# Attention and routed experts in one kernel: unordered stores, moved sums, and a new filling of the steps

## The chip, the cores and the metric

The kernel runs on one core of one Trainium2 chip. The metric is the device time of one execution in microseconds (us). Five engines run their own queues in order: TensorE (PE, with its weight loads as PEld), VectorE (DVE), ScalarE (ACT), GpSimd (POOL) and SyncE (SP, which here only issues DMAs). They wait for each other through semaphores.

## The reference

x has the shape (4, 1024, 512); there are 16 heads of 32, and 8 experts of rank 64. All is float32. B, the experts' second matrix, has the shape (8, 512, 64), A (8, 64, 512).

```python
q, k, v = x @ wq.T, x @ wk.T, x @ wv.T          # in 16 heads, no scaling of the scores
a = softmax(q @ k^T) @ v                        # over 1024 keys, each batch and head
x = layernorm(x + a @ wo.T)
logits = x @ Wr.T + br                          # 8 experts
e, w = argmax(softmax(logits)), max(softmax(logits))
y = (x @ A[e].T) @ B[e].T / 64                  # the chosen expert alone
x = layernorm(x + y * w)
```

## The kernel before

**Steps.** A unit is one batch and one group of four heads, 16 units. The kernel is a written list of 272 steps (and a rest that runs after them). In step i, `scores(i)` takes four matmuls of 128 queries by 512 keys, one head each, for a unit that is 16 steps (`NS`) ahead of the one weighed; DVE takes the maximum of each (L321), and for half of the rows, in the odd steps, ACT also sums the exponentials (L324, one pass over 512 columns for each head). `weigh(i - 16)` computes transposed scores for two blocks of 128 keys and 256 queries: first the row maximum (and, where the sum is known, its logarithm's counterpart for the division) is put into the banks by matmuls of three bf16 parts (L370), then the scores are added (L379), then ACT writes the exponentials, `probs` (L389). Four such steps (`KP`) cover the 1024 keys of 256 queries; in the last of them, a "busy" step (i % 4 == 3), `combine` multiplies with v (L431).

**Two ways to the sum.** Of each eight steps (`TS`), the first four (i % 8 < 4) have no sums from `scores`: GpSimd adds up `probs` into `dens` (L394, L397, eight parts, 2.36 us each), and four steps after the product `settle` sums over the partitions with a matmul by ones (L405), divides (L406) and multiplies (L408). The other four steps (`summed_early`) take the sums of the exponentials that ACT made during `scores`: `pick` matmuls spread the inverse (L417), it is copied to `inv` (L425), and the product is multiplied with it (L440). Both fall in steps 7 mod 8, `settle` first. At the end of the eight `scores` steps the maxima are gathered (L335 to L337: a reduction, a subtraction and an exponential of 16 columns), in the next step `invert` makes the inverse (L343 to L345) and GpSimd splits it into three bf16 parts; two steps later `turn_m` transposes it (L352).

**Banks.** All PE results go through eight PSUM banks in a ring (`bank()`): a step takes four for `weigh`, four for `scores`, one for each piece. A matmul waits until the last reader of its bank is done.

**Pieces.** Projections (q, k, v: L283, L293, L302; output: L503), expert steps and the dense feed-forward of the last batch are pieces with a cost, a first and a last step. A planner walks through the steps and takes pieces, those that are due first, until the step's length passes a level; the level was 1500 above the mean in i % 4 == 1 and 750 below it elsewhere. Work that follows a piece is put into later steps with `later` (small work, after `scores` and `combine`, ahead of the pieces). After the list is made, `keep_order` fixes each engine's order as written.

**After attention.** For batches 0 to 2 (`After`), the normed rows are sorted by expert: `choose` and `gate` find the expert, `count` (L556 to L600) each row's place, `scatter` (GpSimd, indirect DMA, L604, eight for each batch) writes the rows to `sorted` in DRAM. Ten expert steps follow, each with up to three parts of different pairs of tiles: `turn_tokens` (L649), `up` (L656), `down` (L665). SP loads tokens and the expert's matrices (`load_tokens` L620, `load_up` L634, `load_down` L639). Then `weigh_y` takes statistics, GpSimd norms (`apply`, L468), and `store` writes the rows to their places in `out` by an indirect DMA from GpSimd (L683, 48 in all). The framework orders two DMAs that write the same DRAM tensor, so each store waits for the one before it. The last batch (`Last`, L739 to L781, four groups of 256 rows) computes all experts densely with a mask, and SP stores it (L791).

Short names below: steps have the matmuls T1 (L370), T (L379), S (L319), AV (L431), set (L405); o is a piece of the output projection; tt, eu, ed are the three parts of an expert step; lt, l1, lu, lm, ld are the last batch's transposes, mask transposes, up, mask and down.

Of the kernel before, what the change touches and what calls it, by code (L numbers as in the profile page):

```python
# [41 lines left out]
def attention_then_experts(  # L42
# [263 lines left out]
    def scores(s):  # L306
# [24 lines left out]
        if here == TS - 1:  # L331

            m = spread_from[i % 2]
            less = work.tile([P, TQ, GH, 2], F32, tag="less", name="less")
            dve.tensor_reduce(m[:, :, :, 0], top[i], axis=AX.X, op=ALU.min)  # L335
            dve.tensor_sub(less, m[:, TQ:, :, 0:1].to_broadcast((P, TQ, GH, 2)), top[i][:, TQ:])
            act.activation(less, less, AF.Exp)  # L337
            room[i] = m, less
# [23 lines left out]
    def weigh(s):  # L362
# [27 lines left out]
        if not summed_early(s):  # L390
            now = [pr[:, k].rearrange("p j q -> p (j q)") for k in range(2)]
            if kp == 0:
                dens[u, c] = work.tile([P, GH * QC], F32, tag="dens", name="dens", bufs=1)
                pool.tensor_add(dens[u, c], now[0], now[1])  # L394
            else:
                for w in now:
                    pool.tensor_add(dens[u, c], dens[u, c], w)  # L397

    def settle(s):
# [4 lines left out]
        for j in range(GH):  # L404
            pe.matmul(ps[j * HD : (j + 1) * HD, :], ones, dens[u, c][:, ts(j, QC)], start=True, stop=True)  # L405
# [4 lines left out]
    def combine(s):  # L410
# [3 lines left out]
        if summed_early(s):  # L414
# [10 lines left out]
            dve.tensor_copy(inv, ps)  # L425
# [73 lines left out]
    def add_projection(b, n, i, half, h, raw):  # L499
# [6 lines left out]
        if half:  # L506
            dve.tensor_add(raw[:, i], ps[:, H2:], vS[b, 1][:, n * TQ + i, H2:])

    class After:
# [107 lines left out]
        def load_tokens(self, k):  # L617
            for i in range(2):
# [61 lines left out]
        def store(self, k):  # L680
            for i in range(2):
                t = self.x[k, i]
                pool.indirect_dma_start(  # L683
# [6 lines left out]
                )  # L690
# [12 lines left out]
    class Last:  # L703
# [26 lines left out]
        def norm(self):  # L730
            for i in range(TQ):
                apply(self.h[i], self.rs, i, pool if self.n < NQ - 1 else act)
# [55 lines left out]
        def finish(self):  # L788
            self.norm()
            for i in range(TQ):  # L790
                sync.dma_start(out[B - 1, ts(TQ * self.n + i, P), :], self.h[i])  # L791
# [6 lines left out]
    SHORTEST = 8800  # L798
    pieces, loads = [], {}
# [21 lines left out]

    def start_of(u):
        return NS * (u + 1)

    for i in range(len(weights)):
# [3 lines left out]
        if kp == KP - 1:  # L829
            base[i + NS] += COST_AV + (QC + 4 * QC if summed_early(i) else 0)  # L830
# [5 lines left out]
    for i in range(len(weights) // TS):  # L836
        later(TS * i + TS, 0, invert, i, where=ahead)
        later(TS * i + TS + 2, 512, turn_m, i)
# [38 lines left out]
    for b, r in enumerate(rest):  # L877
# [7 lines left out]
        for t in range(NT):  # L885
            n, i = divmod(t, TQ)
            for half in range(2):
                then = []
                if i == TQ - 1 and half == 1:
                    then = [(1, 0, r.norm, n), (3, 0, r.choose, n), (4, 0, r.gate, n)]  # L890
                    if n == NQ - 1:
                        then += [(4, 600, r.count)]
                        then += [(5 + k // 4, 0, r.scatter, k) for k in range(NT)]
# [9 lines left out]
        for k in range(NT + 2):  # L903
# [3 lines left out]
                end + 12 + 3 * k,  # L907
                end + (20 + 4 * k if b < B - 2 else 19 + 3 * k),
                after=[(p, 3 if k else 9)],
# [13 lines left out]
    for n in range(NQ):  # L923
        a = start_of(LAST) + NS * n + NS - 1
        p, ups, downs = None, [], []
        for i in range(TQ):
            for half in range(2):
                then = []
                if i == TQ - 1 and half == 1:
                    gap = 1  # L930
                    then = [(gap, 0, on_last(n, "norm")), (gap + 1, 2200, on_last(n, "turn"))]
                    then += [(gap + 1, 0, on_last(n, "choose")), (gap + 2, 0, on_last(n, "weigh"))]
                    then += [(gap + 2, 300, on_last(n, "turn_one"))]
# [9 lines left out]
        for k in range(C):  # L943
            ups.append(Piece(on_last(n, "up", k), HALF, a + 4, a + 12, after=[(p, gap + 2)]))
        q = Piece(on_last(n, "mask"), 1024, a + 6, a + 14, after=[(p, gap + 3)] + [(o, 1) for o in ups])
# [10 lines left out]
    for i in range(len(base)):  # L956
# [23 lines left out]

        level += 1500 if i % KP == 1 else -750
        length = base[i]
        while True:
# [8 lines left out]
            for gap, cost, f, *args in p.then:  # L992
                later(i + abs(gap), cost, f, *args, where=ahead if gap < 0 else small)
# [16 lines left out]
    for r in rest:  # L1010
        for k in range(NT):
            early[r.steps[k].step - 2].append(lambda r=r, k=k: r.load_tokens(k))
# [26 lines left out]
    for i in range(len(base)):  # L1039
# [8 lines left out]
        if i in busy:  # L1048
            if summed_early(i - NS):
# [45 lines left out]
```

## Time and profile before

| | |
|---|---|
| median of 3 runs | 1541.05 us (1538.18 to 1541.54) |
| profiled execution | 1541.39 us; its span 1539.4 us, mean granted clock 0.989 |
| PE busy | 1493.6 us (97%) |
| DVE, ACT, POOL busy | 1008.9, 946.4, 772.3 us |
| largest groups on DVE, ACT, POOL | L321 maxima 636.1; L389 exponentials 529.2, L324 347.8; L397 additions 452.8 |
| HBM | 92.34 MB read, 33.63 MB written, 82 GB/s over the span |

A profile's instruction row reads: start, busy time, engine, line, operation, what it writes <- what it reads, partitions x elements, count; in brackets the engine's idle time ahead of it and what ended that. A PE matmul of float32 stands as two records. In the waits view a row names who waited for whom: total us, times, longest. Idle time on an engine that nobody waits for costs nothing.

### The profile page before, as it was taken

To read this page: it belongs to the slowest core of one execution; us is meant where nothing else is said; L and a number is where in the kernel's file an instruction comes from. 1 tells how busy PE (TensorE), PEld (TensorE's weight loads), DVE (VectorE), ACT (ScalarE), POOL (GpSimd) and SP (SyncE) were. 2 spreads that over 40 slices of the span, in tenths; PEclk is the share of its full clock that TensorE was granted. 3 is DMA by queue.
4 is the path that set the end of the run, shared out by engine and by line. 5 is a ranking of instruction groups with operands and counts; after the bars stand their busy time and mean duration, and the time that the engine had idled before them with its cause. 6 is when DMAs were issued, how large, how long until landed. Compare 5 with 4: busy or idle time off the path is not lost.

```text
span 1539.4 us, 37695 instructions
## 1 busy us (share of the span) xinstructions
PE 1493.6 (97%) x14899; PEld 972.3 (63%) x14899; DVE 1008.9 (66%) x2117; ACT 946.4 (61%) x2267; POOL 772.3 (50%) x809
## 2 busy tenths in 40 slices
PE   8999999999999999999999999999999999989997
PEld 6676666666665656666666666666666666656665
DVE  3766666666776667677777657777776667776523
ACT  1346677767665676766665676766565577666651
POOL 2013444444556345666644546665555645477651
PEclk9999999999999999999999999999999999999999
DMA  6422121223001513422111513342500231231000
GB/s 233 138 94 72 56 84 43 70 94 114 2 1 49 173 47 114 133 81 98 29 56 37 177 57 90 108 148 64 165 15 28 93 102 36 75 108 34 20 11 28
DMA packets 93056, 122.12 MB, mean 79 GB/s; under 512 B 7607, under 2 KB 68039, under 8 KB 92880
## 3 DMA queue, kind: packets, MB, share of 16 engines
q1 hardware_dynamic: 84672, 103.93, 21.3%
q0 software_dynamic: 6096, 13.69, 2.4%
q8 instruction: 117, 1.92, 0.5%
q10 hardware_dynamic: 2112, 2.10, 0.4%
q14 instruction: 59, 0.48, 0.1%
HBM read 92.34 MB, written 33.63 MB: 82 GB/s over the span
## 4 chain that ended last, share of the span: by engine, by line
PE 85%; ACT 5%; issue 4%; DVE 2%; POOL 2%; DMA 1%; SPq 0%; ACTq 0%; POOLq 0%; DVEq 0%
PE bank L431 15%; PE bank L319 14%; PE bank L379 14%; PE bank L283 8%; PE bank L302 8%; PE bank L293 8%; PE bank L503 6%; PE bank L370 5%; ACT probs L389 4%; PE bank L762 2%; PE bank L777 1%; ACT junk L324 1%; PE bank L665 1%; PE bank L656 1%; POOL dens L397 1%
## 5 line engine op out<-in xcount | busy, mean ns | idle before, releaser
L321 DVE TENSOR_REDUCE top<-bank 128x1 f32<-128x512 f32 x1024 | 636.1, 683 | 318.3 <-PE bank L319 303.4
L389 ACT ACTIVATE probs<-bank 128x512 f32<-128x512 f32 x1024 | 529.2, 605 | 414.0 <-PE bank L379 405.9
L397 POOL TENSOR_TENSOR dens<-dens,probs 128x1024 f32<-128x1024 f32 x192 | 452.8, 2358 | 86.0 <-ACT probs L389 77.1
L324 ACT ACTIVATE junk<-bank,top 128x512 bf16<-128x512 f32 x512 | 347.8, 717 | 76.1 <-DVE top L321 75.9
L319 PE MATMUL bank<-k,q 32*128 32x512 f32 x2048 | 316.2, 600 | 2.5 <-DVE whose_i L600 1.2
L379 PE MATMUL bank<-q,k 32*128 32x256 f32 x4096 | 274.4, 378 | 1.1 <-issue 1.1
L431 PE MATMUL bank<-probs,v 128*32 128x256 f32 x4096 | 237.9, 384 | 4.7 <-ACT probs L389 3.9
L211 POOL CAST sm<-sf 128x32 bf16<-128x32 f32 x32 | 8.2, 256 | 423.5 <-DVE sf L345 404.0
L379 PEld LDWEIGHTS bank<-q,k 32*128 32x128 f32 x4096 | 204.8, 186 | 22.8 <-issue 7.5
L431 PEld LDWEIGHTS bank<-probs,v 128*32 128x32 f32 x4096 | 128.3, 111 | 114.3 <-ACT probs L389 32.3
L319 PEld LDWEIGHTS bank<-k,q 32*128 32x128 f32 x2048 | 129.3, 186 | 37.2 <-DVE aT L440 6.9
L283 PE MATMUL bank<-xT,wq 128*128 128x256 f32 x512 | 130.8, 402 | 10.4 <-DMA xT<-in_xt 7.6
L283 PEld LDWEIGHTS bank<-xT,wq 128*128 128x128 f32 x512 | 96.5, 197 | 53.3 <-ACT probs L389 23.7
L293 PE MATMUL bank<-xT,wk 128*128 128x256 f32 x512 | 125.2, 389 | 0.3 <-ACT probs L389 0.3
L503 PE MATMUL bank<-wo,aT 128*128 128x264 f32 (+1 forms) x512 | 122.7, 390 | 2.4 <-ACT probs L389 2.4
L302 PE MATMUL bank<-wv,xT 128*128 128x256 f32 (+1 forms) x512 | 124.4, 391 | 0.0
L370 PE MATMUL bank<-mT,ones_b 3*128 3x512 bf16 x1024 | 115.7, 386 | 6.1 <-ACT junk L324 5.0
L324 ACT ACTIVATION_READ_ACCUMULATOR junk<-bank,top 128x1 f32 x512 | 121.5, 237 | 0.0
L302 PEld LDWEIGHTS bank<-wv,xT 128*128 128x128 f32 x512 | 93.8, 190 | 38.4 <-ACT probs L389 22.1
L293 PEld LDWEIGHTS bank<-xT,wk 128*128 128x128 f32 x512 | 95.2, 191 | 35.9 <-ACT probs L389 22.4
L503 PEld LDWEIGHTS bank<-wo,aT 128*128 128x128 f32 x512 | 94.2, 190 | 37.0 <-ACT probs L389 22.9
L370 PEld LDWEIGHTS <-ones_b 3*128 3x128 bf16 x1024 | 28.6, 91 | 97.8 <-issue 97.2
(137 smaller groups left out, 1142.9 us busy)
## 6 DMA issues: line engine op xcount, KB each, us to landing
xT<-in_xt SPq DMA_DIRECT2D x98, 512.0 KB, 4.0
sorted<-nothing SPq DMA_DIRECT2D x12, 1028.0 KB, 6.6
x<-sorted SPq DMA_DIRECT2D x48, 257.0 KB, 2.8
h<-in_x SPq DMA_DIRECT2D x32, 256.0 KB, 7.4
wa<-in_wa SPq DMA_DIRECT2D x48, 128.0 KB, 2.1
wb<-in_wb SPq DMA_DIRECT2D x48, 128.0 KB, 3.7
out<-h SPq DMA_DIRECT2D x8, 256.0 KB, 3.6
wv<-in_wv ACTq DMA_DIRECT2D x2, 512.0 KB
```

The costliest lines, as they stand in the source:

```text
L283: pe.matmul(ps, wq_sb[:, c, ts(units[u][1], P)], x.x[:, c, :], start=(c == 0), stop=(c == C - 1))
L293: pe.matmul(ps, wk_sb[:, c, ts(units[u][1], P)], x.x[:, c, :], start=(c == 0), stop=(c == C - 1))
L302: pe.matmul(ps, x.x[:, c, ts(t, P)], wv_sb[:, c, columns(h)], start=(c == 0), stop=(c == C - 1))
L319: pe.matmul(ps, q[r, ts(t % TQ, P)], kT[u][r, ts(n, 512)], start=True, stop=True)
L321: dve.tensor_reduce(top[i][:, at, j, n : n + 1], ps, axis=AX.X, op=ALU.max, negate=True)
L324: act.activation(junk[:, j % 2, :], ps, AF.Exp, bias=top[i][:, at, j, n : n + 1], accum_out=sums[i][:, at - TQ, j, n : n + 1],)
L370: pe.matmul(ps.rearrange("p (k q) -> p k q", q=QC), ones_b[r, :], m[r, :].unsqueeze(1).to_broadcast((NP, 2, QC)), start=True, stop=False,)
L379: pe.matmul(ps[:, ts(k, QC)], kT[u][r, ts(2 * kp + k, P)], qT[u, c][r, :], start=False, stop=(k == 1),)
L389: act.activation(pr[:, :, j, :], ps.rearrange("p (k q) -> p k q", q=QC), AF.Exp)
L397: pool.tensor_add(dens[u, c], dens[u, c], w)
L431: pe.matmul(ps[j * HD : (j + 1) * HD, :], v[:, k, col : col + HD], probs[u, c, k // 2][:, k % 2, j, :], start=(k == 0), stop=(k == NK - 1),)
L503: pe.matmul(ps, aT[b, c, n][:, ts(i, P)], wo_sb[:, c, columns(half)], start=(c == 0), stop=(c == C - 1))
```

## The change

- `store` and `finish` declare that no store to `out` depends on another one.
- The gathering of the maxima and sums becomes `gather`, put into the step's small work: behind `settle` and `combine` on every engine's queue.
- `inv` is copied by ACT instead of DVE.
- The scatters are put two to a step, into steps in which GpSimd adds nothing.
- In the last 256 queries of the last batch, GpSimd adds six of the eight parts; `settle` takes the other two by matmuls of its own (12 instead of 4) and runs one step after the product.
- The planner's level is a fixed 10900 in steps 1 mod 4 (room for two pieces) and the mean elsewhere.
- Expert steps start 5 steps later (ends and gaps change too), their tokens are loaded one step ahead instead of two; in the last batch the transposes come 2 or 3 steps after the projection instead of 2, and the norms of its third group go from GpSimd to ACT.

```diff
-        if here == TS - 1:
-
-            m = spread_from[i % 2]
-            less = work.tile([P, TQ, GH, 2], F32, tag="less", name="less")
-            dve.tensor_reduce(m[:, :, :, 0], top[i], axis=AX.X, op=ALU.min)
-            dve.tensor_sub(less, m[:, TQ:, :, 0:1].to_broadcast((P, TQ, GH, 2)), top[i][:, TQ:])
-            act.activation(less, less, AF.Exp)
-            room[i] = m, less
+    def gather(i):
+
+        m = spread_from[i % 2]
...
+        room[i] = m, less
...
-                for w in now:
+                for w in now[: added(u, c) - 2 * kp]:
                     pool.tensor_add(dens[u, c], dens[u, c], w)
+
+    def added(u, c):
+
+        return NK if u < LAST or c < NQ - 1 else NK - 2
...
-        for j in range(GH):
-            pe.matmul(ps[j * HD : (j + 1) * HD, :], ones, dens[u, c][:, ts(j, QC)], start=True, stop=True)
+        others = range(added(u, c), NK)
+        tiles = [probs[u, c, k // 2][:, k % 2] for k in others]
+        tiles.append(dens[u, c].rearrange("p (j q) -> p j q", q=QC))
+        for w in tiles:
+            for j in range(GH):
+                pe.matmul(
+                    ps[j * HD : (j + 1) * HD, :], ones, w[:, j, :], start=(w is tiles[0]), stop=(w is tiles[-1])
+                )
...
-            dve.tensor_copy(inv, ps)
+            act.copy(inv, ps)
...
+    stores = []
+
+    def stored(i):
+
+        for other in stores:
+            tc.declare_no_dep(i, other, reason="other rows")
+        stores.append(i)
...
-                pool.indirect_dma_start(
+                i = pool.indirect_dma_start(
                     out=out_rows,
...
-                )
+                ).ins
+                stored(i)
...
-                apply(self.h[i], self.rs, i, pool if self.n < NQ - 1 else act)
+                apply(self.h[i], self.rs, i, pool if self.n < 2 else act)
...
-                sync.dma_start(out[B - 1, ts(TQ * self.n + i, P), :], self.h[i])
+                stored(sync.dma_start(out[B - 1, ts(TQ * self.n + i, P), :], self.h[i]).ins)
...
+    HEAVY = 10900
...
+    def quiet(i, k):
+
+        for j in range(i, i + 4 * NS):
+            k -= summed_early(j)
+            if k < 0:
+                return j
...
-            base[i + NS] += COST_AV + (QC + 4 * QC if summed_early(i) else 0)
+            base[i + NS] += COST_AV
+            if summed_early(i):
+                base[i + NS] += QC
+            elif added(u, c) == NK:
+                settled_later.add(i + NS)
+                base[i + NS + KP] += 4 * QC
+            else:
+                later(i + NS + 1, 3 * 4 * QC, settle, i)
...
+        later(TS * i + TS - 1, 0, gather, i)
...
-                        then += [(5 + k // 4, 0, r.scatter, k) for k in range(NT)]
+                        then += [(lambda i, k=k: quiet(i + 5, k // 2), 0, r.scatter, k) for k in range(NT)]
...
-                end + 12 + 3 * k,
-                end + (20 + 4 * k if b < B - 2 else 19 + 3 * k),
-                after=[(p, 3 if k else 9)],
+                end + 17 + 3 * k,
+                end + (25 if b < B - 2 else 21) + 4 * k,
+                after=[(p, 3)] if k else [],
...
-                    gap = 1
-                    then = [(gap, 0, on_last(n, "norm")), (gap + 1, 2200, on_last(n, "turn"))]
-                    then += [(gap + 1, 0, on_last(n, "choose")), (gap + 2, 0, on_last(n, "weigh"))]
-                    then += [(gap + 2, 300, on_last(n, "turn_one"))]
+                    gap = 3 if n < 2 else 2
+                    then = [(1, 0, on_last(n, "norm")), (lambda i, g=gap: i + g + (i + g in busy), 2200, on_last(n, "turn"))]
+                    then += [(gap, 0, on_last(n, "choose")), (gap + 1, 0, on_last(n, "weigh"))]
+                    then += [(gap + 1, 300, on_last(n, "turn_one"))]
...
-        level += 1500 if i % KP == 1 else -750
+        if i % KP == 1 and i < len(maxima):
+            level = max(level, HEAVY)
...
-            early[r.steps[k].step - 2].append(lambda r=r, k=k: r.load_tokens(k))
+            early[r.steps[k].step - 1].append(lambda r=r, k=k: r.load_tokens(k))
...
-            if summed_early(i - NS):
+            if i - KP in settled_later:
                 settle(i - NS - KP)
             combine(i - NS)
```

More of the change, by code (lines that the diff above doesn't have):

```diff
@@ L330, in scores @@
                 )
-        if here == TS - 1:
-            m = spread_from[i % 2]
-            less = work.tile([P, TQ, GH, 2], F32, tag="less", name="less")
-            dve.tensor_reduce(m[:, :, :, 0], top[i], axis=AX.X, op=ALU.min)
-            dve.tensor_sub(less, m[:, TQ:, :, 0:1].to_broadcast((P, TQ, GH, 2)), top[i][:, TQ:])
-            act.activation(less, less, AF.Exp)
-            room[i] = m, less
+    def gather(i):
+        m = spread_from[i % 2]
+        less = work.tile([P, TQ, GH, 2], F32, tag="less", name="less")
+        dve.tensor_reduce(m[:, :, :, 0], top[i], axis=AX.X, op=ALU.min)
+        dve.tensor_sub(less, m[:, TQ:, :, 0:1].to_broadcast((P, TQ, GH, 2)), top[i][:, TQ:])
+        act.activation(less, less, AF.Exp)
+        room[i] = m, less
     def invert(i):
@@ L617, in load_tokens @@
         def load_tokens(self, k):
+            assert len(self.scatters) == NT
             for i in range(2):
@@ L820, in later @@
         where[i].append(lambda: f(*args))
+    def quiet(i, k):
[3 more added lines that the diff above has]
+                return j
     def start_of(u):
         return NS * (u + 1)
+    settled_later = set()
     for i in range(len(weights)):
@@ L943, in attention_then_experts @@
         for k in range(C):
-            ups.append(Piece(on_last(n, "up", k), HALF, a + 4, a + 12, after=[(p, gap + 2)]))
-        q = Piece(on_last(n, "mask"), 1024, a + 6, a + 14, after=[(p, gap + 3)] + [(o, 1) for o in ups])
+            ups.append(Piece(on_last(n, "up", k), HALF, a + 4, a + 12, after=[(p, gap + 1)]))
+        q = Piece(on_last(n, "mask"), 1024, a + 6, a + 14, after=[(p, gap + 2)] + [(o, 1) for o in ups])
         first = a + 7 if n != NQ - 2 else N + 2
@@ L992, in attention_then_experts @@
             for gap, cost, f, *args in p.then:
-                later(i + abs(gap), cost, f, *args, where=ahead if gap < 0 else small)
+                if callable(gap):
+                    later(gap(i), cost, f, *args)
+                else:
+                    later(i + abs(gap), cost, f, *args, where=ahead if gap < 0 else small)
     fill = {i: [p for p in pieces if p.step == i] for i in range(len(base))}
```

## The prediction

> **What bounds the kernel now.** I read the page first, then the timeline by engine for one eight-step period, the starts of all L370 rows (each step from 16 on opens with four such matmuls, so the distance between two openings is a step's time), the waits, and the granted clock by windows. The page:
>
> ```profile
> span 1539.4 us, 37695 instructions
> PE 1493.6 (97%) x14899; PEld 972.3 (63%) x14899; DVE 1008.9 (66%) x2117; ACT 946.4 (61%) x2267; POOL 772.3 (50%) x809
> PE 85%; ACT 5%; issue 4%; DVE 2%; POOL 2%; DMA 1%; SPq 0%; ACTq 0%; POOLq 0%; DVEq 0%
> ```
>
> PE sets the time, and no other engine is near it. So only two things can move the total: PE work, which this edit hardly changes, and places where PE stands still or runs at half clock. I looked for these step by step. A projection piece takes 1.83 to 1.93 us of PE, a product step (3 mod 8) 5.64 us in all, a step 4 mod 8 with one piece 3.98, an odd step with two pieces 5.70 to 5.75. Against these, three kinds of excess stand out.
>
> First, every step after a product with division (0 mod 8). Steps 63 and 64, DVE, then PE's weight loads:
>
> ```profile
> 343.52 0.19 DVE L335 TENSOR_REDUCE sf<-top 128x16 f32<-128x32 f32 x1
> 343.74 0.18 DVE L336 TENSOR_TENSOR less<-sf,top 128x16 f32<-128x16 f32 x1
> 343.83 1.76 DVE L406 RECIPROCAL bank<-bank 128x256 f32<-128x256 f32 x1
> 345.63 0.42 DVE L408 TENSOR_TENSOR aT<-bank,both 128x256 f32<-128x256 f32 x1
> 345.97 0.41 DVE L425 COPY inv<-bank 128x256 f32<-128x256 f32 x1
> 346.52 0.42 DVE L440 TENSOR_TENSOR aT<-bank,inv 128x256 f32<-128x256 f32 x1
> ...
> 347.00 0.29 PEld L319 LDWEIGHTS bank<-k,q 32*128 32x128 f32 x2 [0.27 <-DVE aT L440]
> ```
>
> The fourth score tile of step 64 needs the bank of the product, and L440 frees it last in a DVE queue. The step took 4.63 us; a step 4 mod 8 with the same content takes 3.98. The waits view has this release 26 times.
>
> Second, what GpSimd's queue does to PE, and the clock:
>
> ```profile
> PEld bank L319 <- DVE aT L440: 6.9, 26, 0.3
> POOL out L683 <- DMA out<-x: 66.9, 23, 6.4
> ...
> 491.27:494.69 3.42, 3.42 (x31) 1.26 (x32) 1.71 (x3) 2.79 (x8) 3.34 (x2) 0.50 0.02 5
> 494.69:501.51 6.82, 5.46 (x72) 2.69 (x64) 0.00 (x0) 0.37 (x1) 5.42 (x6) 1.00 0.38 144
> 501.51:508.34 6.83, 4.94 (x20) 3.53 (x24) 2.70 (x5) 2.17 (x4) 3.16 (x4) 0.50 0.43 164
> ```
>
> (In a window's row: length, busy time with instructions of PE, PEld, DVE, ACT, POOL, then granted clock, DMA share, GB/s.) Steps 91 and 92 took 9.92 and 10.19 us instead of 5.64 and 3.98: counting held DVE, PE waited 1.20 us, the clock halved, and eight scatters ran meanwhile. Half clock covers 27.3 us before the last layer norm, in six stretches of 3.41 or 6.83 us.
>
> Third, the end. GpSimd's order decides there, and the clock falls after each wait:
>
> ```profile
> 1374.46 0.98 POOL L683 DMA_INDIRECT out<-x  x1 [3.05 <-DMA out<-x]
> 1377.27 1.53 POOL L468 TENSOR_SCALAR h<-h,rs 128x512 f32<-128x512 f32 x2
> ...
> 1378.10 1.87 PE L739 MATMUL bank<-ident,h 128*128 128x128 f32 x8 [3.34 <-POOL h L468]
> ...
> 1458.81 4.77 POOL L397 TENSOR_TENSOR dens<-dens,probs 128x1024 f32<-128x1024 f32 x2
> ...
> 1463.64 0.72 PE L405 MATMUL bank<-dens,ones 128*32 128x256 f32 x8 [3.21 <-POOL dens L397]
> ```
>
> A store that waits for the store before it delays a norm, and PE waits 3.34 us (step 246: 8.37 us). In step 262, empty of pieces, PE waits for the last addition: 12.39 us.
>
> **The change part by part.** The profiled execution took 1541.39 us (span 1539.4, 2.0 around it), 0.34 above the median of the runs, 1541.05; I sum against 1541.39.
>
> *Gathering behind the products, inv on ACT.* DVE's queue in 7 mod 8 loses 0.31 us ahead of the reciprocal (343.52 to 343.83) and the copy before L440 (345.97 to about 346.3). L440 is then free to start at about 345.66, after the product's end (345.42), and ends at about 346.08; the scores of the next step open at 346.44, so the wait goes. Next late there is nothing: the step should take what 4 mod 8 takes, 3.98. Steps 24 to 248 are 29 such steps, and with two pieces or an expert step the distance is the same (6.33 to 5.75, 5.78 to 5.16): 29 x (4.62 - 3.98) = -18.6. The slack is 0.36 us. The moved rows (L335, L336, L337 on ACT) come some 2.6 us later but still before the inverting rows they feed (346.86). ACT takes 32 x 0.41 us of copies, behind the summed exponentials, in steps where it idles 1.67 us; without that cover it is 13 us, the lower bound of this part is then -5.
>
> *Two pieces in steps with summed exponentials.* I laid the new order of PE over the step times of the old one. Odd step, one piece, then even step, one piece: 3.97 + 5.27 (ACT's 2.06 + 2.75 us run over into the even step, and the bank ring holds PE). Two and one: 5.73 + 4.35. So the second piece costs 1.76 in the odd step and gives back 0.92 in the even one. An even step with scores and no piece (46, 66, 70, 246) has no clean row; bounds are the 2.05 us of its own matmuls and 4.35 with one piece. From ACT's queue (first exponential 1.3 us into the odd step, then 2.06 + 2.75 + about 0.6 until the next step's first bank is free) I take 2.7, near the 3.08 of step 222 with its transposes, and then 0.9 more in the product step behind it. Steps 40 to 71, the same 26 pieces: 158.5 now, 156.9 by these rows, without the gathering. Steps 72 to 159 get 7 pieces more, steps 160 to 215 get 7 fewer; at 1.85 each they cancel, and the rows leave +1.2 and +3.6, mostly from expert steps that now stand in even places. Sum +3, bounds -4 and +8. The experts' token loads are issued one step later, on SP ahead of the xT loads as before; they land in 2.8 us, under a step of at least 4 us. Without that cover it would be 24 x about 1 us.
>
> *Scatters two to a step.* On GpSimd's queue nothing stands between them: in the new order the eight of each batch follow the last addition in one run (1.28 us apart, as at 495.47 to 505.6 now), and the waits in front of them are met. So they are not paced; they only leave the additions. Excess now, count included: steps 90 to 93 11.5, steps 153 to 156 4.5, steps 217 to 221 7.8, together 23.8. The second fours at 862.6 and 1225.9 cost nothing that shows, beside projections; those beside products did. The new runs lie beside projections, mostly. Bounds per batch: 2 (the count alone: steps 153 and 154 took 2.0 more than their kind) and 11.5 (the first batch again). I take 5, near the second batch: 15 - 24 = -9.
>
> *Stores free of each other.* 66.9 us of GpSimd waits go, but additions wait for GpSimd on the path only at the end; elsewhere PE never waits for it. The cover is that GpSimd is busy 50%. SP's queue loses the 81.8 us that `out<-h` waited; no load behind it was late.
>
> *The end, steps 232 to 267.* Expert steps leave the product steps (239: 9.67 us, 251: 9.21, against 6.57 and 5.64 empty), L739 no longer waits in 246 and 247 (8.37 + 7.72, then about 3 + 6.6), step 262 loses about 9 of its 12.39 because two of eight additions (2 x 2.36 us) go to PE and one norm (1.53) to ACT. Added: expert steps that stood before 255 stand after it (6.3 us of PE, no change in the sum) and sixteen small matmuls (2 x 0.9). Step 238, 9.14 us, has DVE's row of reductions, statistics and masks before it; it keeps that, and step 254 now gets the same. In sum, steps 232 to 267 take 198.4 now and about 190 then, of which 1.9 is counted above: -6 (0 to -12). The tail after 268 is paced by ACT (four times 2.06) and then the chain of norms: 0. The later summing there hides: nothing waits for it but a reciprocal with 5 us to spare.
>
> Sum: -18.6 + 3 - 9 - 6 = -30.6; 1541.4 - 30.6 = 1511.
>
> *A rule against the rows.* PE's longest gap in the 3.41 us before the fall at 491.27 is 1.20 us, and the half-clock stretch after it costs 1.7 us.
> The Trainium skill ("TensorE: Matmul & The Clock Gate", "What's actually happening") has the clock fall only after about 3.4 us without work; by it neither that gap nor the emptied steps would cost clock, and the sum would be nearer 1506. The trace shows otherwise.
>
> **Rivals.** *The wait is replaced* (1527): ACT's copy or later splitting on GpSimd takes L440's place, so of 18.6 only 5 come, and the pieces cost +6: 1541.4 - 5 + 6 - 9 - 6 = 1527; with scatters as dear as now 1536. For: slack of only 0.36 us. Against: the banks' other users are done at 345.1.
>
> *The clock stays up* (1496): the 27.3 us at half clock, which cost 13.7, all go. Of these 5.1 (first batch) and 3.4 (third) are in the 23.8 already and 5 at the end; the scatters then cost only their counts, 6 for 15, and step 238 its kind, another 6: -15.
>
> *Indirect DMAs in close order hold PE up* (slower, 1551): 48 stores now run in pairs, 24 scatters in eights. In the first batch a scatter cost about 1.2 us ((11.5 - 2) / 8); at 628.4, 672.4 and 1033.2 the product beside a single store ended about 0.55 us late. My sum holds 9 us for scatters and 5 for stores. If each of the 72 cost 0.75 us, it is 54 instead of 14: 1511 + 40 = 1551. It turns the sign from 0.62 us each ((30.6 + 14) / 72). Against: the fours at 862.6 cost nothing.
>
> *It doesn't do what it says*: holds for the pacing of scatters, and is in the sum.
>
> **How the numbers follow.** My forecast 0.62; replaced wait 0.17; clock stays up 0.14; slower 0.07. A measurement tells about 0.2% (3 us) from no change. Range: from the clock case to near the replaced wait with dear scatters, 1495 to 1533; the slower case lies outside. Faster 0.90, same 0.03 (upper end of the replaced wait), slower 0.07.
>
> **What would show it.** Right: steps 0 mod 8 with one piece at 4.0 us, no release of L319's weight loads by the product's multiplication; eight scatters 1.28 us apart and no more than 5 us excess around them; no GpSimd wait for `out<-x`; no PE wait for `dens` at the end. Wrong: steps 0 mod 8 still at 4.6, or a new releaser there; half clock in more than six stretches; PE slow beside pairs of stores.

## The result, and the profile after

The changed kernel takes 1552.17 us (median of 9 runs, 1544.15 to 1553.26) against 1539.84 us before (9 runs): ratio 1.0072, 95% interval 1.0054 to 1.0090, so it is slower by 12 us where 30 less was predicted. Its profile comes from a run of 1545.04 us (span 1543.3), one of two that fell near 1545 at a mean granted clock of 0.988; the other seven lie between 1551 and 1554 at 0.981 to 0.983.

The page of the changed kernel, the three lines that were shown of before:

```profile
span 1543.3 us, 37686 instructions
PE 1487.5 (96%) x14931; PEld 966.8 (63%) x14931; DVE 997.4 (65%) x2085; ACT 960.4 (62%) x2303; POOL 761.3 (49%) x801
PE 83%; ACT 7%; issue 4%; DVE 3%; DMA 1%; POOL 1%; another core or an unknown queue 1%; ACTq 0%; SPq 0%; POOLq 0%; DVEq 0%
```

PE is busy 6.1 us less, and the span is 3.9 us longer: PE stands more. "Another core or an unknown queue" is new; it stands for waits that end in `remote`, such as those of ACT and DVE in step 221 below.

The first excess is gone. DVE in the timeline at steps 63 and 64 of the changed kernel (343.52 to 346.52 before):

```profile
342.42 1.76 DVE L416 RECIPROCAL bank<-bank 128x256 f32<-128x256 f32 x1
344.21 0.42 DVE L418 TENSOR_TENSOR aT<-bank,both 128x256 f32<-128x256 f32 x1
344.64 0.42 DVE L450 TENSOR_TENSOR aT<-bank,inv 128x256 f32<-128x256 f32 x1
344.99 0.18 DVE L335 TENSOR_REDUCE sf<-top 128x16 f32<-128x32 f32 x1
```

L450, the old L440, ends at 345.06, ahead of the score weights of step 64, which load at 345.32 without a wait. Step 64 takes 3.98 us, as predicted. The waits view has no release of L319 by `aT` any more.

The second excess grew. The third batch's eight scatters, timeline of the changed kernel in step 221:

```profile
1221.78 0.97 POOL L622 DMA_INDIRECT sorted<-h,slot_i  x1 [0.30 <-issue]
1222.02 1.03 PE L379 MATMUL bank<-q,k 32*128 32x256 f32 x16
...
1226.91 0.98 POOL L622 DMA_INDIRECT sorted<-h,slot_i  x1 [0.30 <-issue]
1229.41 2.06 ACT L389 ACTIVATE probs<-bank 128x512 f32<-128x512 f32 x4 [8.13 <-remote]
1229.52 2.49 DVE L321 TENSOR_REDUCE top<-bank 128x1 f32<-128x512 f32 x4 [5.41 <-remote]
...
1230.06 6.34 PE L283 MATMUL bank<-xT,wq 128*128 128x256 f32 x14 [4.77 <-ACT probs L389]
```

PE's transposed scores stand in the trace as done at 1223.05 (ends of matmuls are modelled there), but ACT and DVE start on them and on the scores only at 1229.4, both together, when the packets of the last scatter have ended. PE has its ring of banks full and waits 4.77 us. This lateness is called the hold-up below. The clock falls for 10.23 us (windows view, same kernel: length, busy time of PE, PEld, DVE, ACT and POOL, then granted clock, DMA share, GB/s):

```profile
1222.60:1226.01 3.41, 2.43 (x20) 0.75 (x12) 0.51 (x2) 0.00 (x0) 2.49 (x4) 1.00 0.47 181
1226.01:1236.24 10.23, 6.18 (x15) 4.94 (x16) 2.91 (x5) 4.74 (x12) 1.57 (x2) 0.50 0.62 206
```

Step 221 took 14.97 us, where two projection pieces make 5.75.

The third excess was traded. GpSimd no longer waits for `out<-x`, and steps 262 and 263 take 8.27 us instead of 12.39; but steps 268 to 270, which had been costed at nothing, take 8.52 us instead of 4.54 (timeline of the changed kernel):

```profile
1490.88 1.77 DVE L416 RECIPROCAL bank<-bank 128x256 f32<-128x256 f32 x1 [15.39 <-PE bank L790]
1492.76 0.42 DVE L418 TENSOR_TENSOR aT<-bank,both 128x256 f32<-128x256 f32 x1
1493.10 1.28 DVE L792 TENSOR_TENSOR lu<-bank,lu 128x512 f32<-128x512 f32 x2
1493.23 0.37 PE L370 MATMUL bank<-mT,ones_b 3*128 3x512 bf16 x1 [1.74 <-DVE aT L418]
1493.83 0.37 PE L370 MATMUL bank<-mT,ones_b 3*128 3x512 bf16 x1 [0.23 <-DVE lu L792]
```

The last `settle` now stands ahead of the last weighing steps. Its bank is freed by a reciprocal of 1.77 us, the mask's two banks by the multiplications queued behind it on DVE (L792), and the ring makes L370 wait for all three.

### The profile page after: what moved, and what is told of

Its sections match the earlier page's. It is cut to its first block, busy times and chain, and to the rows that moved or that the text cites. A ratio compares the mean times of both kernels' runs of the same rounds, so it can differ in the third digit from the quotient of the medians.

```text
span 1543.3 us, 37686 instructions
## 1 busy us (share of the span) xinstructions
PE 1487.5 (96%) x14931; PEld 966.8 (63%) x14931; DVE 997.4 (65%) x2085; ACT 960.4 (62%) x2303; POOL 761.3 (49%) x801
## 4 chain that ended last, share of the span: by engine, by line
PE 83%; ACT 7%; issue 4%; DVE 3%; DMA 1%; POOL 1%; another core or an unknown queue 1%; ACTq 0%; SPq 0%; POOLq 0%; DVEq 0%
PE bank L441 15%; PE bank L379 14%; PE bank L319 13%; PE bank L283 8%; PE bank L302 8%; PE bank L293 7%; PE bank L513 7%; ACT probs L389 5%; PE bank L370 5%; PE bank L782 2%; ACT junk L324 2%; PE bank L797 2%; DMA xT<-in_xt 1%; PE bank L684 1%; DVE top L321 1%
## 5 line engine op out<-in xcount | busy, mean ns | idle before, releaser
L397 POOL TENSOR_TENSOR dens<-dens,probs 128x1024 f32<-128x1024 f32 x188 | 443.4, 2358 | 92.5 <-ACT probs L389 83.8
L319 PE MATMUL bank<-k,q 32*128 32x512 f32 x2048 | 303.9, 598 | 4.6 <-DVE whose_i L618 3.3
L319 PEld LDWEIGHTS bank<-k,q 32*128 32x128 f32 x2048 | 121.0, 185 | 36.1 <-issue 7.5
L370 PE MATMUL bank<-mT,ones_b 3*128 3x512 bf16 x1024 | 119.8, 385 | 10.2 <-ACT junk L324 6.0
L370 PEld LDWEIGHTS <-ones_b 3*128 3x128 bf16 x1024 | 29.4, 91 | 103.8 <-issue 103.6
```

The source lines that it names most:

```text
L319: pe.matmul(ps, q[r, ts(t % TQ, P)], kT[u][r, ts(n, 512)], start=True, stop=True)
L370: pe.matmul(ps.rearrange("p (k q) -> p k q", q=QC), ones_b[r, :], m[r, :].unsqueeze(1).to_broadcast((NP, 2, QC)), start=True, stop=False,)
```

## The chips differ

One finding of the experiments comes first, since all readings depend on it. The runs were made on at least five chips, and the kernel before takes about 1540 us on some of them (here: kind I; the runs above are of that kind) and about 1530 us on the others (kind II). The runs of kind I were all made before those of kind II, and no chip was used in both groups; that it is the chip, and not something that changed in between, is likely but not shown. Step times (opening to opening, from the first matmul of `scores` on) of five profiles, in us; the columns II were taken in the runs `before_again`, `after_timed` and `e6_oldlevel` below, "pieces" are projection and dense pieces in before / changed / old level:

| steps | pieces | before, I | before, II | changed, I | changed, II | changed with old level, II |
|---|---|---|---|---|---|---|
| 0-39 | 56/56/56 | 201.64 | 201.63 | 200.43 | 200.43 | 200.42 |
| 40-71 | 26/26/26 | 158.53 | 158.54 | 156.08 | 156.07 | 155.98 |
| 72-87 | 16/22/16 | 86.90 | 86.90 | 92.78 | 92.77 | 85.72 |
| 88-95 (scatters) | 8/10/8 | 52.41 | 45.65 | 51.53 | 48.68 | 45.13 |
| 96-151 | 50/50/48 | 307.94 | 307.80 | 310.21 | 307.05 | 302.43 |
| 152-159 (scatters) | 10/9/11 | 48.65 | 46.15 | 52.59 | 46.96 | 47.64 |
| 160-215 | 56/49/54 | 315.91 | 315.91 | 306.64 | 305.79 | 309.78 |
| 216-223 (scatters) | 8/8/9 | 49.49 | 49.36 | 52.98 | 45.24 | 44.14 |
| 224-267 | | 240.94 | 242.85 | 239.57 | 240.64 | 242.87 |
| 268-270 | | 4.54 | 4.53 | 8.52 | 7.35 | 7.34 |
| 271 to the end | | 48.00 | 48.00 | 47.94 | 47.93 | 47.92 |

Up to step 87, where no indirect DMA has run yet, the two profiles of one kernel in this table agree to 0.01 us. (A third of the changed kernel, `after_again`, takes 154.73 us in steps 40 to 71, where it lacks a half-clock stretch of 3.41 us that the other two have.) Beside scatters they differ by up to 7.7 us. Below, ratios are to runs of before on the same chip; "eights" are the eight scatters of a batch in one run, "pairs" two stores in a row, and "pieces" are counted as in the table.

## The experiments

Theory A: indirect DMAs in close order hold PE up, and the gathering's gain is given back there. Rivals: B, the refilled steps cost the time; C, the clock falls after emptied steps; D, the gathering itself costs elsewhere.

**`e1_gather`** (kind I): before, with the gathering moved and `inv` on ACT.

```diff
-        if here == TS - 1:
+    def gather(i):
...
-            dve.tensor_copy(inv, ps)
+            act.copy(inv, ps)
+        later(TS * i + TS - 1, 0, gather, i)
```

> The kernel before with one part of the change alone: the gathering of sums behind the products, with inv copied by ScalarE. Theory A (indirect DMAs issued in close order hold TensorE up; the gathering is worth its full gain): the steps 0 mod 8 fall from 4.6 to 4.0 us as they did in the changed kernel, and nothing else moves, so about 1539.8 - 18 = 1522 us, ratio 0.988. Theory B (the refilled steps cost the time): the same number, since no step is refilled here. Theory D (the gathering itself takes back elsewhere what the steps 0 mod 8 win, by ScalarE or by a lower granted clock): 1536 us or more.

1523.89 us, ratio 0.9893 (0.9875 to 0.9910). Its step times are 16.7 us below those of before, 13.9 of it in the 29 steps 0 mod 8. The gathering's term was nearly right; D falls.

**`e2_paced`** (kind I): the changed kernel, scatters made to wait.

```diff
+        newest[0] = pr
...
+            if t % 2 == 0:
+                pool.tensor_copy(paced, newest[0][:, 1, GH - 1, QC - 1 :])
             i = pool.indirect_dma_start(
```

> The changed kernel with its scatters really two to a step: ahead of every second scatter GpSimd copies one column of the newest exponentials, so it waits for ScalarE of that step. Theory A: the three windows of steps 88-95, 152-159 and 216-223 lose most of their excess (in the changed kernel 13, 10 and 15 us over steps of 4.0), no step in them is over 6.5 us, and the time falls by 10 to 25 us from the changed kernel's 1552, to 1527-1542. Theory B (the cost is in the refilled steps): those windows lose at most 3 us in sum and the time is 1549-1554.

1534.03 us, ratio 0.9964 (0.9949 to 0.9978), 18 us under the changed kernel. The three scatter stretches take 48.86, 47.00 and 45.22 us, 16.0 less in sum than in the changed kernel's profile, and the half clock beside the third batch is 3.4 us instead of 10.2. Steps 90, 155 and 219 stay at 8.97, 9.97 and 9.91 us, so the bound of 6.5 us was wrong there. On kind II the changed kernel takes 8.94, 9.97 and 9.97 in them (`after_timed`), so this is not the hold-up. It is `count`, once in each batch, and where the clock falls behind it that too (waits view of this kernel):

```profile
PEld bank L321 <- DVE whose_i L621: 5.8, 3, 2.0
```

**`e3_ordered`** (kind I): the changed kernel with stores waiting for each other again.

```diff
-            tc.declare_no_dep(i, other, reason="other rows")
+            pass
```

> The changed kernel with its stores in order again: each waits for the one before it, as in the kernel before, and all else is as changed. Theory A: the late completions of TensorE beside pairs of stores (about 1.1 us each, some 17 pairs in the profile) and the half-clock stretches that follow them go; 8 to 20 us less than the changed kernel, 1532-1544. Theory B: no less than 1549; with the waits of GpSimd for the store before it (66.9 us in the profile of before) back, the end can be up to 5 us longer, 1557.

1545.49 us (1541.57 to 1555.16), ratio 1.0035 (1.0019 to 1.0051): between the two theories. In the trace steps 108, 116, 124 and 183, beside pairs, become 3.6 us shorter in sum (the first three fall from 5.0 to 4.0), and nothing else of A's 8 to 20 us shows; most of the 24 pairs cost nothing. On kind II these four steps are shorter by the same amounts with free stores (`after_timed`).

**`e5_level`** (kind I): before with the new level alone.

```diff
-        level += 1500 if i % KP == 1 else -750
+        if i % KP == 1 and i < len(maxima):
+            level = max(level, HEAVY)
```

> The kernel before with the planner's new level alone (two pieces in the steps that sum exponentials, none in many of those between); stores, scatters and gathering as before. Theory A: within 5 us of before, 1535-1545. Theory B (even steps left without a piece let TensorE stand and the clock fall, two-piece steps run over 9 us): 8 us or more above before, 1548 or more.

1553.33 us, ratio 1.0096 (1.0081 to 1.0112). The number is B's, the place is not: up to step 231 the profile is 0.9 us over before, and steps 256 to 263 then lose 14.1. Step 260 alone takes 14.37 us, with 17.1 us of half clock (waits view of this kernel, 1436 to 1490):

```profile
PE bank L739 <- POOL h L468: 11.2, 1, 11.2
```

With pieces gone to earlier steps, the transposes of the third group of the last batch come due while GpSimd still adds and has not normed their rows. The change has these norms on ACT, so this run says little on the level in the changed kernel.

**`e9_oldlevel`** (kind I) says more: e2_paced with that line of the planner put back.

```diff
-        if i % KP == 1 and i < len(maxima):
-            level = max(level, HEAVY)
+        level += 1500 if i % KP == 1 else -750
```

> e2_paced (1534.0) with the planner's old level: a piece in most steps instead of two in those that sum exponentials. Theory B (refilled steps cost about 8 us by step 216 and more at the end): 1521-1527. Theory A alone (only scatters and stores cost): 1531-1537.

1523.71 us, ratio 0.9886 (0.9866 to 0.9906): the level costs 0.8%, about 10 to 12 us. B holds too.

**`e7_paced_before`** and **`e10_free`** (kind I): e1_gather with the change's scatter places (`quiet`), paced as in e2_paced, its later expert steps and its token loads (one step ahead); then the same with free stores (`stored`).

```diff
 e1_gather, then:
-    then += [(5 + k // 4, 0, r.scatter, k) for k in range(NT)]
+    then += [(lambda i, k=k: quiet(i + 5, k // 2), 0, r.scatter, k) for k in range(NT)]
...
+            if t % 2 == 0:
+                pool.tensor_copy(paced, newest[0][:, 1, GH - 1, QC - 1 :])
...
-                end + 12 + 3 * k,
+                end + 17 + 3 * k,
...
-            early[r.steps[k].step - 2].append(lambda r=r, k=k: r.load_tokens(k))
+            early[r.steps[k].step - 1].append(lambda r=r, k=k: r.load_tokens(k))
...
 e10_free, besides:
-                pool.indirect_dma_start(
+                i = pool.indirect_dma_start(
...
+                stored(i)
```

> The kernel before with the gathering moved (1523.9 by itself), the scatters of the change really two to a step (paced by a one-column copy of the newest exponentials), and the experts' steps placed as late as the change places them, since the scatters end later; old level of pieces, ordered stores, old end. Theory A (scatters in close order are what is given back; paced they bring what the prediction took, 9 us): 1523.9 - 9 = 1515, 1511-1519. Rival B (the scatters cost the same wherever they stand, and the paced kernel gained 18 us over the changed one by some other effect): 1521-1526.

> As e7_paced_before, and the stores free of each other too. Theory A (a pair of stores 1.3 us apart holds TensorE up by about 1 us where it lies beside products): 24 pairs, half of them beside work that waits, so 8 to 20 us more than e7_paced_before. Rival B (free stores cost little; they take GpSimd's 67 us of waits away): within 4 us of it, or up to 5 less at the end.

e7_paced_before: 1528.07 us, ratio 0.9919 (0.9901 to 0.9937), slower than e1_gather and above both expectations. Up to step 223 its profile is 16.5 us ahead of e1_gather's (8.4 of it in steps 88 to 95); from 224 on the later expert steps meet the old end and give back 18, with one wait of PE for tokens (`x<-sorted`) of 5.4 us in step 244. e10_free: 1523.27 us, ratio 0.9881 (0.9862 to 0.9901), so free stores gain 5 us where A said they cost 8 to 20. The trace has both signs: steps 120 to 135 and 176 to 191 lose 4.4 us beside pairs (1.0 to 1.2 each), and from step 240 on, where norms queue behind stores, 10 come back.

**`e8_lateset`** (kind I): e2_paced, GpSimd adding all eight parts again.

```diff
-        return NK if u < LAST or c < NQ - 1 else NK - 2
+        return NK
```

> e2_paced (1534.0) with the last two sums added by GpSimd again as in the kernel before: no early settling of the last products, no probabilities summed by TensorE. If the early settling pays, the wait of TensorE for dens in step 263 comes back (3.2 us and 3.4 us at half clock): 5 to 9 us more, 1539-1543. If, as step 270 suggests (4.28 us instead of 1.08, behind the reciprocal of 1.77 us on VectorE), it costs about what it saves: 1532-1536.

1531.29 us, ratio 0.9937 (0.9917 to 0.9957), 0.3% under e2_paced. The sums by PE, which were to lose step 262's wait, do not pay: steps 264 to 270 take 23.04 us instead of 27.83.

**`e12_two`** (kind II): e1_gather with the paced scatters and later expert steps in the first two batches only.

```diff
-    then += [(lambda i, k=k: quiet(i + 5, k // 2), 0, r.scatter, k) for k in range(NT)]
+    if b < B - 2:
+        then.append((lambda i, k=k: quiet(i + 5, k // 2), 0, r.scatter, k))
+    else:
+        then.append((5 + k // 4, 0, r.scatter, k))
```

> e1_gather (1523.9) with the scatters of the first two batches two to a step and paced, and the experts' steps of these batches as late as in the change; the third batch and the end as in e1_gather. Theory A: the gain of the paced batches stays (in e7_paced_before 10.9 us by step 160, less where pieces move) and the end of e1_gather is kept: 1511-1517. Rival (what the paced scatters give is taken back by pieces that move to the end, whatever the end's rules): 1522-1528.

1520.87 us, ratio 0.9935 (0.9919 to 0.9951). Missed: on this chip there was nothing for pacing to save. It gains less than the gathering gave on kind I, and the trace shows one reason: the third batch's tokens. PE waits for them in step 222 (timeline of this kernel), which takes 8.82 us instead of e1_gather's 4.09:

```profile
1216.02 1.94 PE L655 MATMUL bank<-ident,x 128*128 128x128 f32 x8 [4.83 <-DMA x<-sorted]
```

**`after_again`** (kind II): the changed kernel, unedited, a second profile.

> The changed kernel unedited, for a second profile: most of its runs lie near 1552, the first profile was one of 1545. Theory A: where the time is near 1552, the additional half-clock stretches begin in steps with scatters or pairs of stores (15 to 20 us more half clock than the first profile's 39.4). Theory C (the clock's falls follow standing time anywhere, the emptied steps above all): they begin in or behind steps without a piece.

1529.71 us, a single run, where before takes 1529.37 on the same chip. Steps 219 to 223 show no hold-up. But steps 98 and 226 take 10.02 and 10.03 us instead of 7.12; both follow a step without a piece (97 and 225, 3.08 us). Windows of this kernel:

```profile
531.50:534.89 3.39, 2.80 (x25) 1.83 (x24) 1.26 (x4) 3.39 (x10) 3.21 (x2) 1.00 0.05 15
534.89:541.70 6.81, 6.81 (x25) 3.84 (x27) 3.06 (x5) 2.75 (x6) 5.90 (x3) 0.50 0.00 0
```

0.59 us of standing in 3.39, and the clock halves for 6.8 us. e3_ordered's profile (1555.16 us) has the same two falls; the changed kernel's first profile has neither. Two of them cost 6 us, about the distance between its runs at 1545 and at 1552. No profile of a run at 1552 exists, so that they make this distance is likely, not shown. The Trainium skill ("TensorE: Matmul & The Clock Gate", "What's actually happening") calls the 3.4 us window free-running, so that the same work can fall differently; that agrees with a fall in one run and none in another. That a whole idle window is needed, as the same section has it, does not: this window was 82% busy, and the one before it 3.40 of 3.40 us.

**`after_timed`, `e6_oldlevel`, `e11_again`** (kind II, one chip), and **`e11_oldlate`** (kind II, another): the changed kernel; the changed kernel with the old level; and that with the last sums late and paced scatters.

```diff
 e6_oldlevel:
-        if i % KP == 1 and i < len(maxima):
-            level = max(level, HEAVY)
+        level += 1500 if i % KP == 1 else -750
 e11, besides:
-        return NK if u < LAST or c < NQ - 1 else NK - 2
+        return NK
+            if t % 2 == 0:
+                pool.tensor_copy(paced, newest[0][:, 1, GH - 1, QC - 1 :])
```

> The changed kernel unedited, on the chip of the three runs beside it. If this chip holds TensorE up beside indirect DMAs (before near 1540): ratio 1.006-1.009. If not (before near 1529): 0.998-1.002, since the level of pieces still costs 10 us and the gathering still gives 16.

> The changed kernel with the planner's old level of pieces alone; scatters in eights, stores free and the new end stay. If the level costs 10 us and the eights cost 18, independently, on a chip with the hold-up: 10 us under the changed kernel, 18 above e9_oldlevel's ratio of 0.9886 (so 1.000). On a chip without it: ratio 0.987-0.991.

> The changed kernel with three parts undone or mended: old level of pieces, old late settling of the last sums, scatters paced. If the three add up (1534.0 - 10.3 for the level - 2.7 for the settling): 1519-1523; if the settling only mattered with the new level: 1523-1526.

> The version with the old level, late settling and paced scatters (ratio 0.9882 on the chip without the hold-up). With the hold-up: what the paced scatters avoid is worth more, pairs of stores cost 1 us each in four to eight places: ratio 0.983-0.988. Without it: 0.987-0.990.

Before took 1532.37 us here. The changed kernel: 1524.94 us, ratio 0.9951 (0.9932 to 0.9969), so on this chip it is faster, and by more than was expected. Old level: 1514.19 us, 0.9877 (0.9857 to 0.9898). e11: 1513.57 us, 0.9874 (0.9856 to 0.9891), and 1511.67 us, 0.9882 (0.9863 to 0.9901) on the other chip (expected in kind I's times, as a ratio 0.986 to 0.989). Eights of scatters in e6_oldlevel cost nothing against paced ones in e11_again. The timeline of after_timed at step 220 and 221, the same instructions some 11 us earlier:

```profile
1210.79 0.97 POOL L622 DMA_INDIRECT sorted<-h,slot_i  x1 [0.30 <-issue]
1211.26 1.03 PE L379 MATMUL bank<-q,k 32*128 32x256 f32 x16
1212.38 2.06 ACT L389 ACTIVATE probs<-bank 128x512 f32<-128x512 f32 x4 [1.91 <-PE bank L379]
1213.18 2.48 DVE L321 TENSOR_REDUCE top<-bank 128x1 f32<-128x512 f32 x4 [1.16 <-PE bank L319]
```

The scatters are 1.28 us apart as before, and the packets of these eight take a mean of 0.14 us in both traces. Here ACT starts 1.12 us after the matmuls open, there 7.39 us. Step 221 takes 5.75 us.

**`before_again`** (kind II): the kernel before, unedited.

> The kernel before unedited, for a second profile. On a chip where it takes about 1530: the steps beside scatters and stores are shorter (88 to 95: 52.4 us in the first profile, at most 49; 216 to 223: 49.5, at most 46), the others the same within 0.1 us. On a chip where it takes about 1540: the first profile again, within 2 us.

1533.84 us. Steps 88 to 95 and 152 to 159 are 6.8 and 2.5 us shorter than on kind I. The third batch is not (49.36 us, where at most 46 was expected), but its excess has another cause: step 220 falls from 11.56 us to 5.70, and steps 222 and 223 rise from 9.94 to 15.74. PE now comes early enough to wait for the tokens (timeline of this run), and the clock halves for 6.83 us:

```profile
1226.81 1.94 PE L649 MATMUL bank<-ident,x 128*128 128x128 f32 x8 [3.91 <-DMA x<-sorted]
```

**`m1_alone`, `m2_alone`, `m3_alone`** (kind II): indirect DMAs beside matmuls and nothing else.

```python
for k in range(n):                      # n = 1, 2, 4, 8; five additions of 128x1024 after each group
    pool.indirect_dma_start(out=rows, out_offset=..., in_=h, in_offset=None, ...)
```

> None of the reference's work: it writes zeros, and beside them six streams of TensorE (as a projection piece; as products of 32 rows; as attention products; as scores), each block of which ScalarE copies out and VectorE then copies one column of, while GpSimd adds 128x1024 tiles with groups of 1, 2, 4 and 8 indirect DMAs of 257 KB between them; two more streams of 32-row products beside groups of 2 and 8 plain DMAs of the same bytes, on GpSimd's queue and on SP's. Theory A: beside the eight in at least one stream TensorE's results reach ScalarE 3 us or more late, beside two about 1 us, beside one under 0.6; beside SP's plain DMAs under 0.5. Rival T (the traffic itself does it): the same beside SP's. Rival N: nothing over 0.5 us anywhere, so it takes more than indirect DMAs and a stream of matmuls.

> As m1_alone (zeros written, none of the reference's work), with the products of 32 rows and the scores in four row groups and four banks as in the kernel. On a chip with the hold-up, theory A: ScalarE's copies beside the eight 3 us or more late in at least one stream, beside two about 1 us, beside one under 0.6, beside SP's plain DMAs under 0.5. On a chip without it, or if it takes more than these: nothing over 0.5 us.

> m2_alone with a longer stream of 32-row products, so that all groups lie inside their streams. On a chip where before takes about 1540: theory A has ScalarE's copies beside the eight 3 us or more late in at least one stream, beside two about 1 us, beside one under 0.6, beside plain DMAs under 0.5; the rival has none late, so that it takes more than indirect DMAs beside a full TensorE. On a chip where before takes about 1530: none late, as in m2_alone.

Nothing was late in any of them. m3_alone within its group of eight, copies every 0.86 us, four to a block:

```profile
144.26 0.48 ACT L101 COPY seen<-bank 128x32 f32<-128x32 f32 x4 [0.38 <-PE bank L96]
144.44 0.97 POOL L118 DMA_INDIRECT rows<-h,place  x1 [0.30 <-issue]
145.13 0.48 ACT L101 COPY seen<-bank 128x32 f32<-128x32 f32 x4 [0.38 <-PE bank L96]
```

All three ran on chips of kind II, so they say no more than the kernels did there. What holds PE's results back on kind I, and why there alone, stays open.

## Why the prediction was wrong, by its own steps

Kind I profiles; "rest" is the changed kernel against e1_gather, so without the gathering. The rest is 20.8 us longer, where the prediction had 12 us shorter: 9.6 in the three scatter stretches (forecast -9), 6.6 in steps 40 to 87, 96 to 151 and 160 to 215 (pieces +3, stores 0), 4.9 from step 224 on (-6).

- **Gathering, -18.6: right in its mechanism, a little large.** 16.7 in step times, 15.8 in medians. The 29 steps gave 13.9, since seven of them (144, 152, 208, 216, 232, 240, 248) gained 0.2 us or nothing. The first rival (the wait is replaced) is out: nothing waits for L450, and DVE's 0.28 us for ACT's `less` lies ahead of nothing that PE needs.
- **Scatters, -9: failed, and it is the largest part.** That pacing was only in the words was right. The price was not: 5 us a batch was taken from the second batch and from fours "beside projections" that "cost nothing that shows". In the rest, the scatter stretches are 9.6 us longer (-0.35, +4.11, +5.86); some 4 of it is the level's (4.0 in these stretches between after_timed and e6_oldlevel, 4.2 between e2_paced and e9_oldlevel). Against really paced scatters the eights cost 16.0 us, 0.67 for each. And projections are no cover: PE reaches them, but its ring of banks is full as long as ACT and DVE do not get the scores before; step 221 holds two.
- **Stores, 0: failed by 3.6 us on this kind.** The place where the work stands decided: pairs beside scores cost about 1.1 us (steps 108, 116, 124), most others nothing. At the end free stores gain about 10 us (e10_free).
- **Two pieces in steps with summed exponentials, +3: about right as a sum over steps 40 to 87, 96 to 151 and 160 to 215 (+2.7 on kind II, with the gathering's gain as e1_gather had it), but by two misses that cancel, so by luck.** The level by itself costs 10.75 us (after_timed against e6_oldlevel), 7.8 of it in these stretches; what else the change does there, costed at nothing, gains 5.1 (e6_oldlevel against before, without the gathering; the expert steps' later places are the likely part, not tried alone). The failed sentence is that the pieces moved, "at 1.85 each they cancel". From e6_oldlevel to after_timed, 10 pieces more in steps 72 to 151 cost 15.2 us, and 8 fewer in 152 to 223 give back 3.6. Rows of after_timed and e6_oldlevel (odd step, even step, product) show why: two pieces, one, none take 5.80 + 4.03 + 6.57. A second piece in the even step makes 5.70 of its 4.03. But a piece less in the odd step gives back only 0.71 (4.02 + 5.10 + 6.57), for ACT's exponentials then hold the even step, and the even step's own gives back 1.17 (4.02 + 2.60 + 7.91). The emptied pair had been forecast as 2.7 and 7.5. In steps 45 to 47, where a half-clock stretch follows the emptied step, the three take 15.87 and give back nothing.
- **The end, -6: failed; against e1_gather steps 232 to 267 are only 0.3 us shorter, and steps 268 to 270 add 4.0.** Step 263 gave 4.1 of the 9 us asked of it; steps 244 and 245, with the same work, took 15.35 us instead of 10.9 (15.18 on kind II, so it is not the hold-up). There the tokens loaded one step ahead, costed at nothing because they land in 2.8 us "under a step of at least 4 us", came too late (their median to landing is 3.8 us in the changed kernel), and a fall of the clock followed at 1366.0 (timeline of the changed kernel):

```profile
1361.86 0.91 SPq L639 DMA_DIRECT2D x<-sorted  x2
...
1364.87 0.63 PE L668 MATMUL bank<-ident,x 128*128 128x128 f32 x4 [1.62 <-DMA x<-sorted]
```

  SP had issued two `out<-h` first. Of the 24 places where tokens are loaded, PE waits for them in this one. Last, "nothing waits for it but a reciprocal" overlooked who is queued behind that reciprocal.
- **The clock.** Eight stretches of half clock against seven, 39.4 us against 36.7 in the profiles. At 0.982 instead of 0.988, a run near 1552 has by estimate some 18 us more of half clock (2 x 0.006 x 1545), half of which is lost time: that would cover the 7 us between profile and median. Falls of the clock followed emptied steps (steps 45 to 47, where PE stands 0.23 us in the 3.41 us ahead of the fall; `after_again`, steps 97 to 99), against the rule that the prediction had weighed.
- **The slower rival** (1551, chance 0.07) named the mechanism and nearly the time, but 72 DMAs at 0.75 us is not how it came: the eights cost 16.0 us and the pairs 3.6, 20 instead of its 54, and the pieces, the end and the clock make up the rest. Over all 72 that is 0.28 for each, under its own turning point of 0.62. The evidence for it, half a microsecond beside single stores, was in the profile; "the fours at 862.6 cost nothing" was taken for more than it was. Single stores did not lengthen the steps behind them by more than 0.08 us (steps 116 and 124, before against before_again).

On one chip of kind II the same change is faster by 0.5% (0.3 to 0.7). There the eights cost nothing, the third batch's wait for tokens goes (steps 216 to 223: 49.36 to 45.24 us), and the gathering's gain stays larger than what the level and the tail cost. The versions without the level have the lowest ratios on both kinds: 0.9881 (e10_free) and 0.9886 (e9_oldlevel) on I, 0.9874 (e11_again) and 0.9877 (e6_oldlevel) on II. But on I the gathering alone (e1_gather, 0.9893) cannot be told from them, so nothing else in the change is shown to pay there.

## What to carry to other kernels

Price a moved piece of work at both ends: where it lands in a full step it costs all of its time, and where it leaves a step that another engine then paces it gives back half or less, and an emptied step may let the clock fall. Before several indirect DMAs are issued in a run, find one run of them in the trace that lies beside the same kind of work, and make "two to a step" a wait, not a place in a list. And time a change of one per cent on more than one chip: here its sign differs between the two kinds.

## What the runs showed of the hardware

- On chips where before takes about 1540 us, ACT and DVE start late on results of PE while a run of indirect DMAs goes on (up to 6.4 us after the modelled end beside eight, about 1.1 us beside a pair); on chips where it takes about 1530 they do not. GpSimd's spacing (1.28 us) and the mean time of the eight's packets (0.14 us) are the same on both. Whether the matmuls end late or only their signals come late is open.
- The clock halved for 6.8 us after a window of 3.39 us with 0.59 us of standing, in some runs and not in others; in the changed kernel's first profile it halved for 3.41 us after a window of 3.41 us with 0.23 us of standing (253.23 to 256.64).
- m1_alone's products of 32 rows in a single row group ran at half clock for 515 us while PE was busy without a gap (window 100 to 160 us: 60.00 us busy, clock 0.50). With four row groups in turn, each into its own bank, m3_alone kept the full clock (window 95 to 150: 55.00 us busy, clock 1.00); that the row groups and not the banks decide was not tried.
